# Linear attention over block means: means of the normed rows and one folded product for keys and for values, in place of means of keys and values

## The chip, the cores and the metric

One Trainium2 chip, and one of its cores. The kernel is one launch that runs a whole stack of layers on 2048 rows of 128 numbers. The time is the device time of one execution in microseconds (us); the profiled execution is a separate one, with its own time. Before the change the median of three runs was 4840.54 us (4836.08 to 4840.71).

## The reference

The change touches one layer of the stack, called Hale in the kernel (the eleventh of its 14 stages), and of it the global half; x below are the normalised rows. Cut to what matters:

```python
q = heads(x @ Wq.T); k = heads(x @ Wk.T); v = heads(x @ Wv.T)      # 16 heads of 8
local_out = local_attention(q, k_loc, v_loc, min(local_window, N))
glob = chunked_causal_linear_attention(q, k, v, chunk=chunk_size)   # level 0
scale_w = jax.nn.softmax(haar_scale)
for lvl in range(num_levels):                                       # levels 1 to 4
    block = 2 ** (lvl + 1)                                          # 2, 4, 8, 16
    k_lvl = causal_block_mean(k, block) @ haar_Wk[lvl].T
    v_lvl = causal_block_mean(v, block) @ haar_Wv[lvl].T
    glob = glob + scale_w[lvl] * chunked_causal_linear_attention(q, k_lvl, v_lvl, chunk=chunk_size)
diff = local_m - glob_m
gate_h = silu(concatenate([x, diff]) @ Wg.T + bg)
alpha = sigmoid(gate_h @ Wgo.T + bgo)
return (alpha * local_m + (1.0 - alpha) * glob_m) @ Wo.T + bo
```

causal_block_mean replaces row i by the mean of the rows from the start of its block up to i. The linear attention puts q and k through elu + 1 (phi), and divides each output by the sum of its weights, at least a small constant. Means, Wk and haar_Wk are all linear, and the mean acts on rows while the weights act on columns, so their order is free.

## The kernel before

*Blocks and units.* The 2048 rows are four blocks b of 512 (BW). The class HaleLinear, after the local attention, works in 20 units (b, l), a block and a level 0 to 4, in that order (`run`). Two generators are stepped against each other: `scores` of a unit, which yields after each of its 8 score tiles, and `keys` of the next unit, stepped once at each of those yields, twice in a level 4 unit, where the next unit's `keys` also has to make the next block's queries. A third, `mix`, which makes gate and output of a finished block, is stepped through the level 0 and 1 units of the block after. A scheduler of the framework turns this order into each engine's queue and may advance an instruction past others; an engine then runs its queue strictly in order.

*keys(b, l).* At level 0 `queries` comes first: three matmuls of the high and low parts (mm3, L148 to L150), phi (L2008 to L2013, then the split into hl_pqh and hl_pql, L142 and L143), DMAs that lay these out for the heads (hl_qs, L2031), and v in natural layout, hl_nat (L2036 to L2038), from which the values of level 0 are copied (L2071). The keys of level 0 are mm3 of the normed rows with Wk. The keys of the levels 1 to 4 are mm3 with hl_wl, the product of Wk and haar_Wk made once at the start (L1957 to L1965), which leaves unaveraged keys of the level in PSUM. A segmented scan on DVE (L2076, with a 0/1 tile hl_seg that restarts the sum at a block's first row) turns these to running sums, hl_km; POOL divides by the count (L2079, hl_inv). Then a yield, phi on hl_km, and 12 DMAs that lay the keys out in hl_KS. The values of a level: `mean` multiplies hl_nat by the averaging matrix hl_avg (L2055) and ACT copies the result (L2057); after the yield that follows phi, four matmuls with hl_bdv, the block-diagonal haar_Wv (L2089), and a copy to hl_V (L2090). Another yield, then four transposes of the keys (L2094), their copy hl_kn (L2096), a yield, and for each of the four chunks of 128 rows: the state's increment (L2103), the product of queries and state so far (L2109), its copy (L2110), the increment masked on DVE (hl_t, L2112, single buffer) and added to the state on POOL (hl_S, L2113).

*scores(b, l).* For four groups g of four heads and two pairs of chunks i2: two score matmuls to a PSUM tile ps_a of which two exist (L2155), masked to the causal part either on DVE (L2163) or, for i2 = 0 of g 0 and 2, by another matmul (L2157) and a Relu on ACT (L2160); then, two tiles later, 8 matmuls with the values (`av`, L2142; the trace lists an fp32 matmul like these as two). After two groups the sums are copied by ACT (hl_u, L2126), transposed (`fin2`, L2132) and added to hl_st on DVE (L2135). At the end DVE takes the maximum with 1e-6 and the reciprocal (hl_r, L2180 and L2181), at the levels 1 to 4 times the level's weight (L2183), and hl_o is the product (L2190), which POOL adds to the block's hl_glob (L2191). In a level 4 unit the next block's queries are spread to hl_QP, one product for each head of a group, on ACT for three groups (L2047) and on DVE for the last (L2049).

*PSUM.* The tag c, used by mm3 and the state's increments, has one bank, the tags b and m share three, a has two tiles of two banks.

Of the kernel before, what the change touches and what calls it, by code (L numbers as in the profile page):

```python
# [13 lines left out]
F32 = mybir.dt.float32  # L14
# [7 lines left out]
P = 128  # L22
# [151 lines left out]
class Stage:  # L174
# [75 lines left out]
    def normed(self, b, key="ln"):  # L250
# [11 lines left out]
        xn = self.lnp.tile([P, 4, P], F32, name=key + "_xn", bufs=1)  # L262
# [19 lines left out]
    lnx = 2  # L282
# [1521 lines left out]
class Hale(Attn16):  # L1804


    lnx, NQ = 4, 2
# [140 lines left out]
class HaleLinear:  # L1948
# [3 lines left out]
    def __init__(self, c, stage):  # L1952
# [4 lines left out]
        wkr = c.load(st, "hl_wkr", (P, P), ins["h_wkr"])  # L1957
        bdk = c.load(st, "hl_bdk", (P, 4, P), ins["h_bdk"])
        pw = c.ps("b")
        nc.tensor.matmul(pw, wkr, bdk.rearrange("p l d -> p (l d)"), start=True, stop=True)  # L1960
        wl = [wp.tile([P, 4, P], F32R, name=f"hl_wl{k}") for k in range(2)]
        raw = st.tile([P, BW], F32, name="hl_wlr")
        nc.scalar.copy(raw, pw)
        c.split(*(t.rearrange("p l d -> p (l d)") for t in wl), raw)
        self.wl = wl  # L1965
# [10 lines left out]
        self.seg = c.load(wp, "hl_seg", (P, 4, BW), ins["h_seg"], dtype=BF16)  # L1976
        self.inv = c.load(wp, "hl_inv", (P, 4, 16), ins["h_inv"])
        self.bdv = c.load(wp, "hl_bdv", (P, 4, P), ins["h_bdv"])
# [41 lines left out]
    def queries(self, b):  # L2020
# [12 lines left out]
        pn = c.ps("m")  # L2033
        for i in range(4):
            s = slice(i * P, (i + 1) * P)
            nc.tensor.matmul(pn[:, s], self.lns[b]["xT"][:, s], self.wvn, start=True, stop=True)  # L2036
        t = wk.tile([P, 4, P], F32, name="hl_nat")
        nc.scalar.copy(t.rearrange("p t d -> p (t d)"), pn)  # L2038
        self.nat[b] = t
# [11 lines left out]
    def mean(self, x, l):  # L2051
        c, nc = self.c, self.c.nc
        pm = c.ps("m")
        for i in range(4):
            nc.tensor.matmul(pm[:, i * P : (i + 1) * P], x[:, i, :], self.avg[:, l, :], start=True, stop=True)  # L2055
        t = self.wk.tile([P, BW], F32, name="hl_mean", bufs=1)
        nc.scalar.copy(t, pm)  # L2057
        return t

    def keys(self, b, l):  # L2060
# [4 lines left out]
        nat, phq = self.nat[b], self.phq[b]  # L2065
        (V, Vh), KS = self.VL[self.n % 2], self.KS[self.n % 2]
        self.n += 1
        pk = c.ps("c")
        if l == 0:
            c.mm3(pk, self.wk_, ln["hl"])  # L2070
# [14 lines left out]
        if l:  # L2085
            yield
            pv = c.ps("m")
            for i in range(4):
                nc.tensor.matmul(pv[:, i * P : (i + 1) * P], vm[:, i * P : (i + 1) * P], self.bdv[:, l - 1, :], start=True, stop=True)  # L2089
# [347 lines left out]
```

## Time and profile before

| what | us |
|---|---|
| median of three runs | 4840.54 |
| profiled execution, its own time | 4829.24 |
| its span, first to last instruction | 4827.3 |
| stretch of HaleLinear in it | about 3195 to 3620 |
| from one unit to the next, block 0 | 17.5 |
| from one unit to the next, levels 2 and 3 of later blocks | 17.8 |
| level 1 of later blocks, beside the tail of mix | 18.9 |
| level 4 and the next level 0 together | 41.3 |

Over the whole span the profile lists PE (TensorE's matmuls) with PEld (its weight loads, which overlap them), DVE (VectorE), ACT (ScalarE), POOL (GpSimd) and SP (the engine that issues the DMAs). The groups give for one line, engine, operation and tile the busy time and mean duration of one instruction, and then the time that the engine stood idle just before, with what ended it. A part of the waits says who waited for whom, how long in total, how often, and the longest. The chain of waits follows the work that ended last back from its end: each piece is what the next one waited for, or ran behind on the same engine. By the chain of the whole span, PE has 68% of it and DVE 21%. In the steady part of the stretch the granted TensorE clock is 1.00 of full speed; in its first 20 us it is 0.61.

### The profile page before, as it was taken

What the parts mean: (1) busy time and instruction counts of PE and PEld (TensorE: products, weight loads), DVE (VectorE), ACT (ScalarE), POOL (GpSimd) and SP (SyncE); (2) the same over time, 40 slices, a digit from 0 to 9 for tenths busy, and PEclk for the clock granted to TensorE, in tenths of its full rate; (3) what the DMA queues carried; (4) which work ended last, traced back from release to release, by engine and by line L of the source; (5) the groups of instructions that cost most, each with busy time, mean ns of one, the idle gap of its engine ahead of it and who ended that gap; (6) DMA issues with size and microseconds to landing.
All of it is one profiled execution on the core that took longest, in us unless ns stands there. A gap on an engine that the chain in (4) does not pass through costs nothing.

```text
span 4827.3 us, 89159 instructions
## 1 busy us (share of the span) xinstructions
PE 4397.6 (91%) x36369; PEld 2493.9 (52%) x36388; DVE 3709.7 (77%) x5694; ACT 3052.3 (63%) x5570; POOL 947.1 (20%) x826
## 2 busy tenths in 40 slices
PE   5979999988699988799999999989988989999998
PEld 4744444655344443463444447756656634444466
DVE  7867887589666654789999958447868879999777
ACT  4634568875355555356888875345546648888866
POOL 4730000554100000330000013012215600000056
PEclk9966899998699999898999999989999969999999
DMA  1010000000000000000000000112211000000000
GB/s 52 4 47 6 4 2 9 23 1 17 17 14 14 18 10 8 8 1 2 2 2 2 2 4 12 33 50 51 52 47 37 9 8 2 2 2 2 2 20 7
DMA packets 69484, 73.33 MB, mean 15 GB/s; under 512 B 17616, under 2 KB 44102, under 8 KB 69076
## 3 DMA queue, kind: packets, MB, share of 16 engines
q1 hardware_dynamic: 69076, 67.64, 5.0%
q8 instruction: 287, 4.70, 0.4%
q14 instruction: 121, 0.99, 0.1%
HBM read 32.09 MB, written 1.05 MB: 7 GB/s over the span
## 4 chain that ended last, share of the span: by engine, by line
PE 68%; DVE 21%; ACT 5%; issue 4%; POOL 1%; DMA 1%; SPq 0%; POOLq 0%; ACTq 0%; DVEq 0%
PE ps_c L874 15%; PE ps_a L824 10%; PE ps_c L1478 5%; DVE at_mx L828 4%; PE ps_b L895 4%; PE ps_c L878 3%; PE ps_a L1438 3%; PE ps_b L1491 3%; PE ps_b L148 2%; PE ps_a L148 2%; PE ps_a L150 2%; PE ps_b L149 2%; PE ps_a L149 2%; PE ps_b L150 2%; DVE m_hl L450 1%
## 5 line engine op out<-in xcount | busy, mean ns | idle before, releaser
L901 ACT ACTIVATE at_P<-ps_b 128x512 f32<-128x512 f32 (+2 forms) x2688 | 1414.4, 581 | 333.7 <-PE ps_b L895 205.6
L828 DVE TENSOR_REDUCE at_mx<-ps_a 128x2 f32<-128x1024 f32 (+2 forms) x1344 | 1537.0, 1183 | 103.7 <-PE ps_b L895 60.2
L874 PE MATMUL ps_c<-at_P,at_V 128*32 128x256 f32 (+3 forms) x10752 | 865.8, 395 | 7.8 <-ACT at_u L883 7.3
L895 PE MATMUL ps_b<-at_q,at_KT 32*128 32x512 f32 (+2 forms) x2688 | 761.0, 499 | 6.6 <-DMA at_q<-at_mT 5.0
L824 PE MATMUL ps_a<-at_KT,at_q 32*128 32x512 f32 (+3 forms) x2688 | 701.5, 522 | 46.9 <-DVE at_mx L828 44.7
L824 PEld LDWEIGHTS ps_a<-at_KT,at_q 32*128 32x128 f32 x2688 | 267.5, 196 | 494.1 <-issue 331.9
L449 ACT ACTIVATE m_hh<-ps_a,moe_b 128x512 fp32r<-128x512 f32 x512 | 350.0, 689 | 193.0 <-DVE m_h L446 160.5
L1439 DVE TENSOR_REDUCE ml_mx<-ps_a 128x2 f32<-128x1024 f32 x256 | 305.0, 1221 | 214.0 <-PE ps_a L1438 213.3
L450 POOL TENSOR_TENSOR m_hl<-m_h,m_hh 128x512 fp32r<-128x512 f32 x256 | 360.2, 1408 | 541.1 <-ACT m_hh L449 531.9
L1493 ACT ACTIVATE ml_P<-ps_b 128x512 f32<-128x512 f32 (+1 forms) x544 | 272.4, 576 | 229.8 <-PE ps_b L1491 227.6
L874 PEld LDWEIGHTS ps_c<-at_P,at_V 128*32 128x32 f32 x10752 | 215.9, 110 | 358.8 <-issue 179.9
L878 PE MATMUL ps_c<-wide,zerob 128*32 128x256 bf16 x5184 | 390.2, 281 | 0.0
L261 POOL TENSOR_TENSOR ln_rs<-ln_ve,nhalf 128x4 f32<-128x4 f32 x56 | 61.6, 1101 | 1656.2 <-DVE ln_ve L259 1647.6
L895 PEld LDWEIGHTS ps_b<-at_q,at_KT 32*128 32x128 f32 x2688 | 326.8, 189 | 74.1 <-issue 44.2
L450 DVE TENSOR_TENSOR m_hl<-m_h,m_hh 128x512 fp32r<-128x512 f32 x256 | 256.9, 1004 | 80.1 <-ACT m_hh L449 78.8
L448 ACT ACTIVATE m_h<-ps_a,moe_b 128x512 f32<-128x512 f32 x320 | 220.7, 690 | 75.3 <-DVE m_hl L450 39.9
L1478 PE MATMUL ps_c<-ml_P,ml_V 128*33 128x512 f32 (+3 forms) x1088 | 253.5, 588 | 2.9 <-ACT ml_P L1493 2.9
L148 PE MATMUL ps_b<-m_hh,moe_w2h 128*128 128x512 f32 x512 | 221.2, 432 | 20.7 <-DVE m_t L470 19.2
L149 PE MATMUL ps_b<-m_hl,moe_w2h 128*128 128x512 f32 x512 | 213.2, 416 | 25.5 <-DVE m_hl L450 20.0
L148 PE MATMUL ps_a<-ln_h,moe_w1h 128*128 128x512 f32 x512 | 219.1, 429 | 11.8 <-ACT m_hh L449 11.7
L878 PEld LDWEIGHTS <-zerob 128*32 128x32 bf16 x5184 | 155.8, 100 | 112.6 <-issue 9.2
L149 PE MATMUL ps_a<-ln_l,moe_w1h 128*128 128x512 f32 x512 | 206.6, 403 | 0.0
(655 smaller groups left out, 7734.6 us busy)
## 6 DMA issues: line engine op xcount, KB each, us to landing
hl_KS<-hl_pkh SPq DMA_DIRECT2D x160, 64.0 KB
moe_w_raw<-in_l0f_W SPq DMA_DIRECT2D x32, 256.0 KB
ml_pad<-ml_QT SPq DMA_DIRECT2D x32, 256.0 KB
moe_w_raw<-in_l3f_W SPq DMA_DIRECT2D x32, 256.0 KB
hl_KS<-hl_pkl SPq DMA_DIRECT2D x80, 64.0 KB
at_pad<-at_q SPq DMA_DIRECT2D x64, 64.0 KB
at_q<-at_mT SPq DMA_DIRECT2D x192, 4.0 KB
at_cosT<-in_cosT SPq DMA_DIRECT2D x8, 256.0 KB
```

The lines of the kernel that those rows point to most:

```text
L148: nc.tensor.matmul(out, lh, rh, start=start, stop=False)
L149: nc.tensor.matmul(out, lh, rl, start=False, stop=False)
L449: nc.scalar.activation(hh, ph, AF.Relu, bias=bias)
L450: (nc.gpsimd if f in ((0, 2) if self.spare else MS) else nc.vector).tensor_tensor(hl, h, hh.bitcast(F32), ALU.subtract)
L824: self.in_turn(nc.tensor.matmul(pa[:, k, :w], q[r, i * P : (i + 1) * P], KT[r, ch * BW : ch * BW + w], start=True, stop=True))
L828: nc.vector.tensor_reduce(mx[:, i, 2 * jj : 2 * jj + 2, ch], pa[:, :, :w], AX.X, ALU.max)
L874: self.in_turn(nc.tensor.matmul(self.acc[32 * j : 32 * j + 32, s], self.V[:, kt, h : h + 32], ps[j][:, s], start=start, stop=stop))
L878: self.in_turn(nc.tensor.matmul(self.acc[32 * j : 32 * j + 32, z], c.zerob, c.wide[:, z], start=False, stop=False))
L895: self.in_turn(nc.tensor.matmul(pbs[k][:, off:end], KT[r, kt * P : (kt + 1) * P], q[r, off:end], start=True, stop=not diag))
L901: nc.scalar.activation(p[:, off:end], pbs[k][:, off:end], AF.Exp, scale=scale)
L1439: nc.vector.tensor_reduce(mx[:, i, :, ch], pa, AX.X, ALU.max)
L1478: self.in_turn(nc.tensor.matmul(self.acc[64 * j : 64 * j + m, s], v, ps[k][j][:, s], start=kt + k == 0, stop=kt + k == NT - 1))
```

## The change

It is one edit of HaleLinear with two helpers. The running means are now taken of the normed rows xn, which the layer norm keeps for all four blocks (lnn = 4 buffers of ln_xn instead of 1), with hl_avg: `means` copies the PSUM result twice on ACT, as the high part hl_meanh (new L2051) and in full (hl_mean, new L2052), and subtracts on DVE for the low part hl_meanl (new L2053). There is a yield after it. The keys of a level are mm3 of these with hl_wl, and go straight to phi; the values are one product of the mean with hl_wvl (new L2075), the product of Wv and haar_Wv, made at the start as hl_wl is. Level 0 has its values from xT and Wv by the same lines, without hl_nat. The scan, hl_seg, POOL's product, hl_inv, and the load of hl_bdv in its old place are gone. The weight of a level moves from hl_r into hl_o, which becomes a product with a scalar and a tensor (new L2179). The loads of the two folds and of Wq and Wk come first.

```diff
@@ -259,7 +259,7 @@
         nc.vector.tensor_scalar_add(ve, mv[:, :, 1], EPS)
         rs = self.sm.tile([P, 4], F32, name=key + "_rs")
         nc.gpsimd.tensor_tensor(rs, ve, c.nhalf, ALU.pow)
-        xn = self.lnp.tile([P, 4, P], F32, name=key + "_xn", bufs=1)
+        xn = self.lnp.tile([P, 4, P], F32, name=key + "_xn", bufs=self.lnn)
         for i in range(4):
             nc.vector.tensor_scalar(xn[:, i, :], c.x[:, 4 * b + i, :], mv[:, i, 0:1], rs[:, i : i + 1], ALU.subtract, ALU.mult)
         return xn
@@ -279,7 +279,7 @@
             r["hl"] = (h, l)
         return r
 
-    lnx = 2
+    lnx, lnn = 2, 1
 
     def top2(self, l, shape=(P, 4, E)):
         c, nc = self.c, self.c.nc
@@ -1804,7 +1804,7 @@
 class Hale(Attn16):
 
 
-    lnx, NQ = 4, 2
+    lnx, lnn, NQ = 4, 4, 2
 
     def open(self):
         c, ins = self.c, self.c.ins
@@ -1954,15 +1954,17 @@
         nc, ins = c.nc, c.ins
         wp = self.wp = stage.pool("hl_w")
         st = stage.pool("hl_s", 2)
-        wkr = c.load(st, "hl_wkr", (P, P), ins["h_wkr"])
-        bdk = c.load(st, "hl_bdk", (P, 4, P), ins["h_bdk"])
-        pw = c.ps("b")
-        nc.tensor.matmul(pw, wkr, bdk.rearrange("p l d -> p (l d)"), start=True, stop=True)
-        wl = [wp.tile([P, 4, P], F32R, name=f"hl_wl{k}") for k in range(2)]
-        raw = st.tile([P, BW], F32, name="hl_wlr")
-        nc.scalar.copy(raw, pw)
-        c.split(*(t.rearrange("p l d -> p (l d)") for t in wl), raw)
-        self.wl = wl
+        raw = {}
+        for n in "kv":
+            w = c.load(st, "hl_wr", (P, P), ins[f"h_w{n}r"])
+            bd = c.load(st, "hl_bd", (P, 4, P), ins[f"h_bd{n}"])
+            pw = c.ps("b")
+            nc.tensor.matmul(pw, w, bd.rearrange("p l d -> p (l d)"), start=True, stop=True)
+            raw[n] = (st if n == "k" else wp).tile([P, 4, P], F32, name=f"hl_w{n}l")
+            nc.scalar.copy(raw[n].rearrange("p l d -> p (l d)"), pw)
+        self.wl = [wp.tile([P, 4, P], F32R, name=f"hl_wl{k}") for k in range(2)]
+        c.split(*self.wl, raw["k"])
+        self.wvl = raw["v"]
         self.wq = c.load_hl(wp, st, "hl_wq", (P, P), ins["h_wq"])
         self.wk_ = c.load_hl(wp, st, "hl_wk", (P, P), ins["h_wk"])
         stage.shut("hl_s")
@@ -1973,9 +1975,6 @@
         self.bgo = c.load(wp, "hl_bgo", (P, 1), bcast(ins["h_bgo"]))
         self.wo = c.load(wp, "hl_wo", (P, P), ins["h_wo"])
         self.bo = c.load(wp, "hl_bo", (P, P), bcast(ins["h_bo"]))
-        self.seg = c.load(wp, "hl_seg", (P, 4, BW), ins["h_seg"], dtype=BF16)
-        self.inv = c.load(wp, "hl_inv", (P, 4, 16), ins["h_inv"])
-        self.bdv = c.load(wp, "hl_bdv", (P, 4, P), ins["h_bdv"])
         self.avg = c.load(wp, "hl_avg", (P, 4, P), ins["h_avg"])
         self.bdm = c.load(wp, "hl_bdm", (P, 16, 9), ins["h_bdm"])
         self.tri = c.load(wp, "hl_tri", (P, P), ins["h_tri"])
@@ -2030,13 +2029,6 @@
             for s, src in enumerate((qh, qh, ql)):
                 nc.sync.dma_start(t[32 * s : 32 * s + 32, :].bitcast(F32), src[32 * g : 32 * g + 32, :].bitcast(F32))
         self.phq[b] = phq
-        pn = c.ps("m")
-        for i in range(4):
-            s = slice(i * P, (i + 1) * P)
-            nc.tensor.matmul(pn[:, s], self.lns[b]["xT"][:, s], self.wvn, start=True, stop=True)
-        t = wk.tile([P, 4, P], F32, name="hl_nat")
-        nc.scalar.copy(t.rearrange("p t d -> p (t d)"), pn)
-        self.nat[b] = t
         yield
 
     def spread(self, g):
@@ -2048,46 +2040,45 @@
             return
         nc.vector.tensor_tensor(self.QP[g], self.qs[g].bitcast(F32).unsqueeze(1).to_broadcast([P, 4, BW]), self.hm.unsqueeze(2).to_broadcast([P, 4, BW]), ALU.mult)
 
-    def mean(self, x, l):
-        c, nc = self.c, self.c.nc
+    def means(self, xn, l):
+
+        c, nc, wk = self.c, self.c.nc, self.wk
         pm = c.ps("m")
         for i in range(4):
-            nc.tensor.matmul(pm[:, i * P : (i + 1) * P], x[:, i, :], self.avg[:, l, :], start=True, stop=True)
-        t = self.wk.tile([P, BW], F32, name="hl_mean", bufs=1)
-        nc.scalar.copy(t, pm)
-        return t
+            nc.tensor.matmul(pm[:, i * P : (i + 1) * P], xn[:, i, :], self.avg[:, l, :], start=True, stop=True)
+        h, l = (wk.tile([P, BW], F32R, name=f"hl_mean{k}", bufs=1) for k in "hl")
+        x = wk.tile([P, BW], F32, name="hl_mean", bufs=1)
+        nc.scalar.copy(h, pm)
+        nc.scalar.copy(x, pm)
+        nc.vector.tensor_tensor(l, pm, h.bitcast(F32), ALU.subtract)
+        return x, (h, l)
 
     def keys(self, b, l):
         c, nc, wk = self.c, self.c.nc, self.wk
         if l == 0:
             yield from self.queries(b)
         ln = self.lns[b]
-        nat, phq = self.nat[b], self.phq[b]
+        phq = self.phq[b]
         (V, Vh), KS = self.VL[self.n % 2], self.KS[self.n % 2]
         self.n += 1
+        if l == 0:
+            x, hl, w, wv = ln["xT"], ln["hl"], self.wk_, self.wvn
+        else:
+            x, hl = self.means(ln["xn"], l - 1)
+            w, wv = tuple(t[:, l - 1, :] for t in self.wl), self.wvl[:, l - 1, :]
+            yield
         pk = c.ps("c")
-        if l == 0:
-            c.mm3(pk, self.wk_, ln["hl"])
-            nc.scalar.copy(Vh[:, :, :, 0:8], nat.rearrange("p t (h d) -> p t h d", d=8))
-        else:
-            c.mm3(pk, tuple(t[:, l - 1, :] for t in self.wl), ln["hl"])
-            vm = self.mean(nat, l - 1)
-            km = wk.tile([P, BW], F32, name="hl_km", bufs=1)
-            nc.vector.tensor_tensor_scan(km, self.seg[:, l - 1, :], pk, 0.0, ALU.mult, ALU.add)
-            pk = km
-            k3 = km.rearrange("p (n s) -> p n s", s=16)
-            nc.gpsimd.tensor_tensor(k3, k3, self.inv[:, l - 1, :].unsqueeze(1).to_broadcast([P, BW // 16, 16]), ALU.mult)
+        c.mm3(pk, w, hl)
+        pv = c.ps("m")
+        for i in range(4):
+            s = slice(i * P, (i + 1) * P)
+            nc.tensor.matmul(pv[:, s], x[:, s], wv, start=True, stop=True)
+        nc.scalar.copy(Vh[:, :, :, 0:8], pv.rearrange("p (t h d) -> p t h d", t=4, d=8))
         yield
         phk, kh, kl = self.phi(pk, "hl_pk")
         for g in range(4):
             for s, src in enumerate((kh, kl, kh)):
                 nc.sync.dma_start(KS[g][32 * s : 32 * s + 32, :].bitcast(F32), src[32 * g : 32 * g + 32, :].bitcast(F32))
-        if l:
-            yield
-            pv = c.ps("m")
-            for i in range(4):
-                nc.tensor.matmul(pv[:, i * P : (i + 1) * P], vm[:, i * P : (i + 1) * P], self.bdv[:, l - 1, :], start=True, stop=True)
-            nc.scalar.copy(Vh[:, :, :, 0:8], pv.rearrange("p (t h d) -> p t h d", t=4, d=8))
         yield
         pt = c.ps("m")
         for i in range(4):
@@ -2179,19 +2170,17 @@
         r = wk.tile([P, 4, 16], F32, name="hl_r")
         nc.vector.tensor_scalar_max(r, st[:, :, :, 8], 1e-6)
         nc.vector.reciprocal(r, r)
-        if l:
-            nc.vector.tensor_scalar_mul(r, r, self.w[:, l - 1 : l])
         bc = r.unsqueeze(3).to_broadcast([P, 4, 16, 8])
         if l == 0:
             self.glob = wk.tile([P, 4, 16, 8], F32, name="hl_glob")
             nc.vector.tensor_tensor(self.glob, st[:, :, :, 0:8], bc, ALU.mult)
         else:
             t = wk.tile([P, 4, 16, 8], F32, name="hl_o", bufs=1)
-            nc.vector.tensor_tensor(t, st[:, :, :, 0:8], bc, ALU.mult)
+            nc.vector.scalar_tensor_tensor(t, st[:, :, :, 0:8], self.w[:, l - 1 : l], bc, ALU.mult, ALU.mult)
             nc.gpsimd.tensor_tensor(self.glob, self.glob, t, ALU.add)
 
     def run(self):
-        self.done, self.phq, self.nat = {}, {}, {}
+        self.done, self.phq = {}, {}
         units = [(b, l) for b in range(NB) for l in range(5)]
         for _ in self.keys(*units[0]):
             pass
@@ -2407,10 +2396,8 @@
     i64 = np.arange(64)[None]
     k128 = np.arange(P)[:, None]
     d["h_maskc"] = np.ascontiguousarray(np.stack([np.where(k128 <= i64, 0.0, -1e30), np.where((k128 <= 64 + i64) & (k128 > i64), 0.0, -1e30)], 1).astype(ml_dtypes.bfloat16))
-    d["h_wkr"] = g("L3_attn_a_Wk")
+    d["h_wkr"], d["h_wvr"] = g("L3_attn_a_Wk"), g("L3_attn_a_Wv")
     t512 = np.arange(BW)[None]
-    d["h_seg"] = np.ascontiguousarray(np.broadcast_to(np.stack([(t512 % B > 0) for B in (2, 4, 8, 16)], 1), (P, 4, BW)).astype(ml_dtypes.bfloat16))
-    d["h_inv"] = f(np.broadcast_to(np.stack([1.0 / (t512[:, :16] % B + 1) for B in (2, 4, 8, 16)], 1), (P, 4, 16)).astype(np.float32))
     d["h_hm"] = f((row[:, None] // 8 == np.arange(4)[None]).astype(np.float32))
     return d
```

## The prediction

> **What bounds the kernel now.** I read the busy shares first, then the busy time by stretch, the groups of the linear-attention stretch, its waits, and the chain of waits through one unit. Line numbers are those of the kernel before; lines of the changed kernel are called new.
>
> ```profile
> span 4827.3 us, 89159 instructions
> ...
> PE 4397.6 (91%) x36369; PEld 2493.9 (52%) x36388; DVE 3709.7 (77%) x5694; ACT 3052.3 (63%) x5570; POOL 947.1 (20%) x826
> ```
>
> PE is busy for 91% of the span. The change touches one stretch only, from 3195 to 3620 us, 9% of the span. The stretches inside it (us; busy us of PE, PE's weight loads, DVE, ACT, POOL; clock; DMA):
>
> ```profile
> core 0: us, PE busy (x) PEld busy (x) DVE busy (x) ACT busy (x) POOL busy (x), PEclk, DMA share, GB/s
> 3195.00:3215.00 20.00, 9.17 (x26) 5.89 (x26) 9.07 (x20) 7.25 (x13) 12.07 (x23) 0.61 0.46 130
> ...
> 3340.00:3420.00 80.00, 73.63 (x822) 50.77 (x821) 65.00 (x102) 43.04 (x76) 18.29 (x24) 1.00 0.21 51
> ```
>
> In the steady part PE is busy 92%, DVE 81%, ACT 54%, POOL 23%. So at most 8% of some 400 us is PE's idle time there, and only the first 20 us are slack. What lies in that idle time shows in the groups (count, busy us and mean ns, then idle before):
>
> ```profile
> L2163 DVE TENSOR_TENSOR hl_am<-ps_a,hl_tri 128x1024 f32<-128x1024 f32 x120 | 146.0, 1216 | 20.6 <-PE ps_a L2155 20.1
> ...
> L2079 POOL TENSOR_TENSOR hl_km<-hl_km,hl_inv 128x512 f32<-128x512 f32 x16 | 22.3, 1396 | 66.0 <-DVE hl_km L2076 53.1 <-DVE hl_r L2180 13.0
> ...
> L2076 DVE TENSOR_TENSOR_SCAN hl_km<-hl_seg,ps_c 128x512 f32<-128x512 bf16 x16 | 19.5, 1217 | 1.9 <-PE ps_c L150 1.9
> ...
> L143 DVE TENSOR_TENSOR hl_pkl<-hl_pk,hl_pkh 128x512 fp32r<-128x512 f32 x19 | 12.9, 679 | 1.9 <-ACT hl_pkh L142 1.9
> ...
> L2183 DVE TENSOR_SCALAR hl_r<-hl_r,hl_sc 128x64 f32<-128x64 f32 x16 | 9.9, 621 | 0.4
> L2057 ACT COPY hl_mean<-ps_b 128x512 f32<-128x512 f32 x16 | 9.3, 584 | 9.9 <-PE ps_b L2055 9.9
> ```
>
> and in the waits (us in total, times, longest):
>
> ```profile
> PEld ps_a L2155 <- DVE hl_am L2163: 21.0, 34, 1.1
> ...
> PE ps_a L2155 <- DVE hl_am L2163: 11.2, 21, 0.9
> ```
>
> The chain that ended last, through the start of one unit (start, us, what):
>
> ```profile
> 3357.61 0.53 DVE hl_st L2135 x2
> ...
> 3358.38 1.15 DVE hl_km L2076
> 3359.53 0.46 DVE hl_r L2181
> ...
> 3360.01 0.99 DVE hl_r L2183
> 3360.99 1.13 DVE hl_am L2163
> 3362.13 0.60 DVE hl_o L2190
> 3362.72 0.34 DVE hl_e L2011
> 3363.06 1.14 DVE hl_am L2163
> ...
> 3364.25 0.50 PE ps_a L2155
> ```
>
> A unit (one block, one level) takes 17.8 us between the same instructions of successive units. DVE carries its first 6.6 us, because the score matmuls L2155 wait for DVE's mask to free their PSUM. PE carries the other 11.2. Summing PE's spacings, I find about 16.0 us of work per unit, so 1.6 to 1.85 us is stall. That is the most an ordinary unit can give.
>
> **The change, part by part.** *Removed*, once per unit of levels 1 to 4, so 16 times: the scan, 16 x 1.217 = 19.5 us of DVE; the product with hl_inv, 22.3 us of POOL; the weight on hl_r, 9.9 us of DVE. In the ordinary unit two of the three stand on the chain above, 1.15 and 0.99 us.
>
> *Added*: the subtraction that makes the low part of the mean (new L2053). No row has this shape with a PSUM source. Between L2135 (PSUM, 144 elements, 0.297) and L2163 (PSUM, 1024, 1.216) a line gives 0.68 for 512; L143, the same operation from SBUF, takes 0.679; I take 0.69, so 16 x 0.69 = 11.0 of DVE. A second ACT copy of the mean, 16 x 0.584 = 9.3. PE's work per unit stays the same: four matmuls for the mean, three for the keys, four for the values, in both. The weight now rides in hl_o, a product with two tensors and a scalar like L2013 (0.677), against 0.683 before.
>
> DVE has 29.4 - 11.0 = 18.4 us less work. If it all came off the path, and the POOL step as well, the gain would be near 30 us.
>
> *Moved*: the mean now stands ahead of the keys, so the chain is mean, ACT copy, key matmuls, phi, where it was key matmuls, scan, POOL, phi. Phi comes a step later in the generator. I walked the changed kernel's order of instructions on each engine with these durations. For an ordinary unit, times run from its first score matmul:
>
> - fin2 ends at 1.6, hl_st on DVE at 2.15, hl_r 2.9, then the second mask until 4.1 (6.2 before, in the unit that starts at 3373.76). hl_o to 4.8, the new subtraction to 5.5, the next masks to 6.7 and 7.9. The third pair's scores, which wait for the first of these, start at about 6.8; before, 8.3. So 1.5 us of the old stall is gone.
> - The mean's matmuls end at 2.4, its ACT copies at 3.05 and 3.65. The last key matmuls wait for the subtraction, until 5.55, and end at 6.3. ACT's two steps of phi end at 7.6, DVE's at 9.0 or a little later (before, 8.85). Keys are thus no earlier, in spite of all that was removed.
> - Then DVE's queue has hl_pk, a mask, hl_pkl, a mask, and only then hl_t (L2112), which frees the one ps_c bank that the next state matmul (L2103) needs. Before, hl_t stood before that last mask. The mask ends at 12.1 to 12.5, hl_t at 12.4 to 12.9; PE, done with all else at 11.4 to 11.7, idles 1.1 to 1.2 us, and 0.35 to 0.6 more for POOL's addition to hl_S (0.49, L2113) behind it.
> - Sum: stall 1.5 to 1.85 again, unit 17.6 to 17.8 against 17.8. I take -0.1, for nine units of this kind (of 20: 3 in the first block, 2 in each other): -0.9.
>
> What is late next, then, is hl_t behind a mask. Its cover before was that mask's later place.
>
> *The three units of level 4 with the queries of the next block, and the level 0 after each* (together 41.3 us before). ACT multiplies hl_QP there (12 x 0.715), with the copy hl_u behind. In the new order the next queries' hl_pq comes after a mask (7.3 against 5.8), the keys' hl_pk at 13.4 against 9.7, and ACT's row of hl_QP is cut by hl_pkh and hl_kn, so that the last hl_u ends near 22.6 against 19.9 and its transposes 2.75 later. In the level 0 unit that follows, ACT no longer waits 2.6 for POOL's product ahead of its mask. The gate's matmul L2239 is 3.1 late, but scores and state matmuls have gone ahead meanwhile: +1.3 for the pair (-1 to +4), three times: +3.9.
>
> *The three level 1 units with the tail of mix* (18.9 before): the key matmuls wait for the addition to x that frees ps_c; I find 18.5 to 20: +0.5 each, +1.5.
>
> *The start*: the wanted weights are now loaded first, before the last attention is over; SP issues a load each 0.47 us, and five stood ahead of hl_wkr. The query matmuls start at about 3198.5 instead of 3200.79. ACT no longer does hl_nat between two steps of phi. And the product on POOL, 3.23 us there at 3220.83, ahead of ACT's first mask, is gone, where PE stood for 6.5 us; the new mean and keys take its place in part. The second fold costs two matmul halves and a copy, 0.58 on ACT, in idle time. I take -2.8 (0 to -6). *The end*: the last unit has nothing beside it and loses the weight, 0.24 to 0.6: -0.4.
>
> Sum: -0.9 + 3.9 + 1.5 - 2.8 - 0.4 = **+1.3 us**. The profiled execution took 4829.24 (span 4827.3), which would become 4830.5. It is 11.3 below the median of the runs, 4840.54, so the forecast there is **4842**, no change. About 0.2%, 9.7 us, is what a measurement of this kernel can tell from no change.
>
> **A rule against the change.** The rows: ACT is busy 54%, and its 0.58 for a copy from PSUM lies in idle time in my walk. The Trainium skill, "Trainium Kernel Development and Optimization", section "Best Practices", warns to mind PSUM pressure, that is evacuation. The mean is read from PSUM three times instead of once; if those reads stood on the path they would cost 16 x (0.58 + 0.69), some 20 us.
>
> **Rivals.**
>
> *A, the stall stays gone.* DVE gets to the masks 1.5 us earlier and the new wait for hl_t is shorter than I find, because hl_t is ready before the mask or the mask comes early enough. For: two removed steps stood on the chain. Against: the new order puts that mask ahead. Then each of 12 ordinary and level 1 units gains up to 1.5, 18 us; with the other terms as above (+3.9 - 2.8 - 0.4) that is -17.3: 4823. Half of it gives 4832.
>
> *B, the longer key chain decides; slower.* Mean, two copies, subtraction, keys, phi: if the subtraction is held behind hl_o and a mask (1.2), hl_pk, its transposes and every hl_t move back by as much, and PE, which has nothing else left by 11.7, idles that much longer. It decides once hl_pk ends after 9.7. At +1.0 in 12 units and +2.7 in the three level 4 units, whose whole delay I counted as half recovered: 12 + 8 - 3 = +17: 4858. Against: the subtraction needs no more than ACT's copy at 3.65, long past when its turn comes.
>
> **How the numbers follow.** Forecast 0.42, within about 8 us of 4842; A 0.28; B 0.30. The bounds: ordinary units -14 to +10, level 4 pairs -3 to +12, level 1 units -3 to +6, start 0 to -6; not all at one end, so some 20 each way: **4820 to 4862**. Faster 0.30 (most of A, and a little of the forecast), within 0.2% 0.38, slower 0.32.
>
> **What would show it.** In the changed profile: the third pair's scores start near 6.8 in a unit (if 8.3, the gain was not there); PE's idle time before L2103 named with hl_t, 1 us and more per unit (if near zero, A); hl_pk ends near 9 to 9.3 in a unit (if 10 or more, B); the level 4 unit's last hl_u near 22.6; the first mask of ACT ends 2 to 4 us earlier than 3228.26. The forecast is wrong if units shrink below 17.0 or grow above 18.5.

## The result, and the profile after

The changed kernel takes 4856.77 us in the median (4850.83 to 4861.43, six runs), the kernel before 4834.93 (4829.03 to 4840.71, six runs). The ratio is 1.0045, 95% interval 1.0035 to 1.0055: slower by about 22 us. The forecast was 4842, no change; the time lies inside the range of 4820 to 4862, near the price of rival B, but "no change" was wrong.

The page of the kernel after; below its span, each engine's busy time, share and instructions. The profiled execution took 4859.93 us.

```profile
span 4858.2 us, 89145 instructions
...
PE 4440.9 (91%) x36390; PEld 2514.1 (52%) x36390; DVE 3694.2 (76%) x5678; ACT 3057.3 (63%) x5583; POOL 928.5 (19%) x810
```

DVE has 15.5 us less work than before and POOL 18.6 less, as the change meant. PE has 43.3 us *more*, with 21 more matmul records of 36,000. Part of that lies elsewhere in the span, which ran at a lower mean clock (0.921 against 0.926). To leave that out I use one measure from here on: *linear time*, from the last transposes of the local attention to the last addition to x. It was 424.8 us and is 446.4: +21.6, as much as the difference of the medians. It is read, like all units below, from one profiled execution of each kernel.

The busy time of the kernel after by stretch (us; busy us of PE, PE's weight loads, DVE, ACT, POOL; clock; DMA):

```profile
3345.00:3402.00 57.00, 54.80 (x592) 37.44 (x594) 40.33 (x68) 25.83 (x50) 7.96 (x13) 1.00 0.17 42
3195.00:3625.00 430.00, 391.75 (x3998) 263.01 (x3997) 289.67 (x498) 215.58 (x385) 73.29 (x119) 0.95 0.20 50
```

And the kernel before, over the same 430 us:

```profile
3195.00:3625.00 430.00, 371.79 (x3993) 256.65 (x3993) 314.41 (x557) 217.22 (x385) 96.52 (x138) 0.94 0.21 53
```

Over three units of block 1, levels 1 to 3, at a full clock in both kernels, DVE's load fell from 81% (3338 to 3391 before) to 71%, and PE's rose from 94% to 96%. PE is busy 20.0 us longer over the 430 us, with 5 more records of 4000. Three groups of the kernel after in that stretch (count, busy us and mean ns, then idle before) show what of the walk came true:

```profile
L2146 PE MATMUL ps_a<-hl_QP,hl_KS 128*128 128x512 f32 x320 | 123.1, 469 | 3.0 <-DVE hl_am L2154 2.8
L2133 PE MATMUL ps_b<-hl_am,hl_V 128*32 128x128 f32 x2560 | 112.5, 281 | 1.4 <-DVE hl_am L2154 1.3
...
L2053 DVE TENSOR_TENSOR hl_meanl<-ps_b,hl_meanh 128x512 fp32r<-128x512 f32 x16 | 10.9, 683 | 4.8 <-ACT hl_mean L2052 4.8
```

And its waits (us in total, times, longest):

```profile
PEld ps_c L2094 <- DVE hl_t L2103: 12.6, 18, 1.2
...
PEld ps_a L2146 <- DVE hl_am L2154: 6.8, 13, 0.9
```

The prices of the new instructions were nearly right: the subtraction 0.683 (0.69 forecast), and by rows not shown the second copy 0.594 (0.584) and hl_o 0.744 (0.677). So was the main effect: the score matmuls' wait for DVE's mask, 21.0 us for the weight loads and 11.2 for the matmuls before, is 6.8 and 2.8, and the wait for hl_t that was named as next is there, 12.6 us for 3.6 before, 1.2 at its longest. The surprise is the value matmuls L2133. There are as many as before (2560), of the same mean, yet they cover 112.5 us. Their row before was:

```profile
L2142 PE MATMUL ps_b<-hl_am,hl_V 128*32 128x128 f32 x2560 | 100.0, 279 | 0.4 <-DVE hl_am L2163 0.4
```

The chain of waits through one ordinary unit of the kernel after (block 1, level 3, from 3383.14 to 3402.31; start, us, what) shows how:

```profile
3389.22 0.34 PE ps_b L2133 x2
3389.56 0.43 PE ps_c L149
3389.99 0.24 PE ps_c L150
3390.22 0.57 PE ps_b L2133 x14
...
3393.16 0.56 PE ps_b L2133 x10
3393.71 0.58 PE ps_b L2085 x4
3394.30 0.25 PE ps_b L2100 x2
3394.54 0.35 PE ps_b L2133 x6
...
3395.59 0.29 DVE hl_am L2154
3395.88 0.85 issue
3396.73 0.31 DVE hl_t L2103
...
3397.08 0.53 PE ps_c L2094 x2
```

Before, the first 6.6 us of such a unit were a chain of DVE instructions. Now nearly every piece is PE's own; the one stall is from 3395.56 to 3397.08, 1.5 us, for the mask and hl_t. And two groups of value matmuls are torn, with the last parts of the key product (L149) and the transposes of the keys (L2085) between their pieces: 2 + 14 records take 0.34 + 0.57, and 10 + 6 take 0.56 + 0.35. A whole group, 16 records, is one piece of 0.57. (A third group is cut 2 + 14 near the end of the unit, but its first two records follow the run before, so no run is added; with what lies between, its pieces take 2.51 us, as the whole ones do in joined below.) In the whole stretch the value matmuls come in 158 runs against 139 before; in an ordinary unit in 9 against 7. That is the scheduler's order: the same value matmuls, placed differently.

The units, from the first score matmul to that of the next (us; a range where units differ), with those of the main experiments:

| part | before | after | joined | joined_pair | split | w_in_o | w_in_o_old | ahead3 |
|---|---|---|---|---|---|---|---|---|
| start to first unit of level 1 | 48.8 | 44.5 | 44.0 | 44.1 | 49.5 | 48.7 | 47.8 | 44.7 |
| block 0, levels 1 to 3 | 17.5 | 18.6 | 17.7 | 17.7 | 18.2 | 17.5-17.8 | 17.5-19.5 | 17.1-17.7 |
| level 1 | 18.9 | 20.6 | 20.0 | 20.0 | 19.7 | 18.9 | 18.9 | 18.6 |
| levels 2 and 3, blocks 1 and 2 | 17.8 | 19.2 | 18.2 | 18.2 | 18.5 | 17.9 | 18.1 | 17.3-17.6 |
| level 4 and next level 0 | 41.3 | 44.2-44.9 | 44.0-45.0 | 43.3-43.8 | 41.9-43.1 | 43.3-44.3 | 41.0-42.6 | 42.5 |
| last unit to x | 35.9 | 35.7 | 35.7 | 35.7 | 36.9 | 35.7 | 35.7 | 36.4 |
| linear time | 424.8 | 446.4 | 435.5 | 432.3 | 437.9 | 433.3 | 431.5 | 421.3 |

The pairs can't be read from this table as they stand. TensorE's granted clock was 0.50 for 6.8 us in each of the three level 4 units of the kernel after; the stretches (columns as before):

```profile
3311.50:3318.30 6.80, 6.13 (x21) 4.73 (x20) 1.92 (x5) 4.18 (x9) 1.50 (x4) 0.50 0.44 106
3417.30:3424.10 6.80, 6.69 (x52) 5.52 (x56) 2.20 (x7) 4.86 (x11) 1.96 (x4) 0.50 0.37 90
3519.70:3526.50 6.80, 6.33 (x34) 4.91 (x38) 1.75 (x6) 4.59 (x11) 1.95 (x4) 0.50 0.41 98
```

All three pairs of joined have one as well (6.8, 6.8 and 3.4 us), two of w_in_o and one each of joined_pair, split and w_in_o_old (3.4 us each); the pairs of the kernel before and of ahead3 have none. Where a run has pairs with and without, a stretch of 3.4 us goes with 0.5 to 1.6 us more. The pairs without one take 41.3 before, 43.4 in w_in_o, 41.0 in w_in_o_old, 43.3 in joined_pair, 41.9 in split and 42.5 in ahead3. For the kernel after and joined there is no such pair, and what theirs would be is not shown; nor is whether the change brings the stretches on.

### The profile page after: what moved, and what is told of

It is laid out like the page before. It is cut to its first block, busy times and chain, and to the rows that moved or that the text cites. A ratio compares the mean times of both kernels' runs of the same rounds, so it can differ in the third digit from the quotient of the medians.

```text
span 4858.2 us, 89145 instructions
## 1 busy us (share of the span) xinstructions
PE 4440.9 (91%) x36390; PEld 2514.1 (52%) x36390; DVE 3694.2 (76%) x5678; ACT 3057.3 (63%) x5583; POOL 928.5 (19%) x810
## 4 chain that ended last, share of the span: by engine, by line
PE 59%; DVE 14%; ACT 4%; issue 3%; POOL 1%; DMA 1%; SPq 0%; POOLq 0%; DVEq 0%; ACTq 0%
PE ps_c L874 12%; PE ps_a L824 8%; PE ps_c L1478 5%; PE ps_a L1438 3%; PE ps_b L1491 3%; PE ps_b L895 3%; DVE at_mx L828 2%; PE ps_c L878 2%; PE ps_b L2133 2%; PE ps_a L148 1%; PE ps_a L2146 1%; PE ps_a L150 1%; PE ps_a L149 1%; PE ps_b L148 1%; PE ps_b L149 1%
## 5 line engine op out<-in xcount | busy, mean ns | idle before, releaser
L895 PEld LDWEIGHTS ps_b<-at_q,at_KT 32*128 32x128 f32 x2688 | 325.5, 188 | 74.2 <-issue 43.8
L448 ACT ACTIVATE m_h<-ps_a,moe_b 128x512 f32<-128x512 f32 x320 | 220.8, 690 | 78.5 <-DVE m_hl L450 42.5
L148 PE MATMUL ps_b<-m_hh,moe_w2h 128*128 128x512 f32 x512 | 222.5, 435 | 20.7 <-DVE m_t L470 17.8
L149 PE MATMUL ps_b<-m_hl,moe_w2h 128*128 128x512 f32 x512 | 214.4, 419 | 25.2 <-DVE m_hl L450 19.5
L878 PEld LDWEIGHTS <-zerob 128*32 128x32 bf16 x5184 | 155.5, 100 | 112.5 <-issue 9.1
L149 PE MATMUL ps_a<-ln_l,moe_w1h 128*128 128x512 f32 x512 | 208.4, 407 | 0.0
```

The costliest lines, as they stand in the source:

```text
L148: nc.tensor.matmul(out, lh, rh, start=start, stop=False)
L149: nc.tensor.matmul(out, lh, rl, start=False, stop=False)
L878: self.in_turn(nc.tensor.matmul(self.acc[32 * j : 32 * j + 32, z], c.zerob, c.wide[:, z], start=False, stop=False))
L895: self.in_turn(nc.tensor.matmul(pbs[k][:, off:end], KT[r, kt * P : (kt + 1) * P], q[r, off:end], start=True, stop=not diag))
```

## The experiments

Three causes were weighed at first: the order of PE's queue, that is the torn runs; L, the longer key chain (mean, copies, subtraction, keys, phi) that now stands in line within a unit; and V, the evacuation, PSUM read three times for a mean. The expectations call the first theory O. To hold an order I add dependences without semaphores between the instructions of one engine, in the sequence of a written list, so that the scheduler can't exchange them; each queue then has exactly that order and no new wait. The kernels below were timed in five rounds on three chips; ratios are to the kernel before on the same chip, with 95% intervals.

**joined.** The changed kernel, its queues held to their own order but for one thing: each group of 8 value matmuls stays whole, at the place of its last piece (the edit is shortened).

```diff
+ORDERS = (PE, DVE, ACT, POOL)          # instruction numbers, one list an engine
+for names in ORDERS:
+    for a, b in zip(names, names[1:]):
+        tc.add_manual_dep(at[b], a, NoSync, reason="order")
```

> The changed kernel with one thing different: in TensorE's queue the eight value matmuls of a group (new L2133), which the changed kernel cuts up and sets between other matmuls, stand together again, each group at the place of its last piece. That makes 130 runs of value matmuls instead of 152. The queues of DVE, ACT and POOL are held to the changed kernel's order. Theory O (the order: a run of value matmuls costs TensorE some 0.3 us to go in and out of, as the spacings show, 0.20 out of it and 0.1 into it): 22 runs less, 5 to 9 us faster than the changed kernel, ordinary units 19.17 to about 18.5 us. Theory L (the key chain is longer through mean, copies and subtraction, and TensorE waits for hl_t): within 2 us of the changed kernel. Theory V (the mean's three reads of PSUM cost ACT and DVE time on the path): within 2 us too.

Measured: 4847.52 us, ratio 1.0022 (1.0006 to 1.0037); linear time 435.5, half of the loss gone, somewhat more than theory O had expected; 136 runs. The same place in the chain of joined, in the same columns:

```profile
3382.47 0.23 PE ps_c L149
3382.70 0.24 PE ps_c L150
3382.94 0.57 PE ps_b L2149 x16
...
3385.88 0.44 PE ps_b L2101 x4
3386.31 0.25 PE ps_b L2116 x2
3386.56 0.57 PE ps_b L2149 x16
...
3388.12 0.85 issue
3388.97 0.31 DVE hl_t L2119
```

In the kernel after, the first torn group cost 0.34 more in itself, and 0.20 more in what followed its first piece (L149 0.43 against 0.23); the second cost 0.34 and 0.14 (the transposes 0.58 against 0.44). Together 1.02, and an ordinary unit is 1.0 shorter. The wait behind mask and hl_t is as long as it was. So the torn groups are half of the loss, nearly all of it in the units of levels 1 to 3, and the rest is something else.

**split.** The opposite, on the kernel before, with its queues held: 64 groups of value matmuls that stood whole behind a pair of score matmuls are cut in the middle. In outline:

```diff
-scores scores value x8
+scores value x4 scores value x4
```

> The kernel before with one thing different: 64 groups of eight value matmuls (L2142), each right behind a pair of score matmuls, are cut in halves that stand behind one score matmul each. Same matmuls, same data, 202 runs of value matmuls instead of 138; the queues of DVE, ACT and POOL are held to the order of before. Theory O: 64 x 0.3 = 19 us at most, 10 to 19 since about half of the cuts lie where TensorE waits for DVE in any case. Theories L and V have no cost in this: 0 to 3 us, for the scores that come a quarter of a us later.

Measured: 4850.00 us, ratio 1.0030 (1.0018 to 1.0041); linear time 437.9, +13.1 for 64 more runs, 0.20 each, within what theory O expected. (One pair has a stretch of half clock, some 1.2 of the 13.1.) Nothing of the change is in this kernel, and it is slower by more than half of what the change cost. In its chain one cut group, with the scores:

```profile
3377.10 0.23 PE ps_a L2171
3377.34 0.36 PE ps_b L2158 x8
3377.69 0.43 PE ps_a L2171
3378.13 0.36 PE ps_b L2158 x8
```

This is 1.38 us, where the chain of the kernel before has the same work whole:

```profile
3384.97 0.47 PE ps_a L2155 x2
3385.43 0.57 PE ps_b L2142 x16
```

That is 1.04, so a cut costs 0.34 where PE leads. Where DVE leads, in the first third of a unit, it is partly hidden, hence 0.20 in the mean.

**w_in_o.** The kernel before with the smallest part of the change alone: the weight moves from hl_r into hl_o, one DVE instruction of 0.62 less for each unit of levels 1 to 4.

```diff
-        if l:
-            nc.vector.tensor_scalar_mul(r, r, self.w[:, l - 1 : l])
-            nc.vector.tensor_tensor(t, st[:, :, :, 0:8], bc, ALU.mult)
+            nc.vector.scalar_tensor_tensor(t, st[:, :, :, 0:8], self.w[:, l - 1 : l], bc, ALU.mult, ALU.mult)
```

> The kernel before with one part of the change alone: the level's weight goes into hl_o (a product with a scalar and a tensor) and its own multiplication on hl_r is gone. Scan and POOL's product stay. By the chain of waits of before it is worth up to 0.7 us in an ordinary unit and less in the others: 3 to 8 us faster than before. If TensorE's order alone sets the time (theory O), 0 to 3 us faster, as the order hardly changes (133 runs). L and V say nothing of this.

Measured: 4842.10 us, ratio 1.0016 (1.0005 to 1.0027); linear time 433.3, +8.5: slower, where 0 to 8 us faster had been expected. Nearly all of it lies in the pairs of level 4 and level 0, which grow from 41.3 to 43.4 at full clock (44.3 in the two with a stretch of half clock). DVE's timeline at the start of a level 4 unit (start, us, what, idle before) tells why:

```profile
3401.74 0.42 DVE L2011 TENSOR_SCALAR hl_e<-hl_e 128x512 f32<-128x512 f32 x1
3402.08 1.22 DVE L2163 TENSOR_TENSOR hl_am<-ps_a,hl_tri 128x1024 f32<-128x1024 f32 x1
3403.21 0.68 DVE L2013 SCALAR_TENSOR_TENSOR hl_pq<-ps_c,hl_e 128x512 f32<-128x512 f32 x1
```

In the kernel before, hl_pq stands ahead of that mask:

```profile
3396.70 0.68 DVE L2013 SCALAR_TENSOR_TENSOR hl_pq<-ps_c,hl_e 128x512 f32<-128x512 f32 x1
3397.30 1.22 DVE L2163 TENSOR_TENSOR hl_am<-ps_a,hl_tri 128x1024 f32<-128x1024 f32 x1
```

With one instruction fewer the scheduler put the mask first, and the next queries, the keys behind them and the last copies all come later. The ordinary units gain nothing either: 17.9 for 17.8. There the scheduler put hl_o ahead of the mask and beside POOL's product, and it takes 1.50 us instead of 0.74.

**w_in_o_old.** The same, with each queue held to the order of the kernel before. In outline:

```diff
+ORDERS = (those of the kernel before, without the instructions on hl_r)
```

> The same instructions as in the run with the weight in hl_o alone, but with the queues of TensorE, DVE, ACT and POOL held to the order of the kernel before (less the 16 multiplications). In that run the pairs of level 4 and the next level 0 took 44.3 us against 41.3 before, although only the weight was moved; its DVE queue has the next queries' hl_pq behind a mask, and ACT's row of hl_QP starts before hl_pkh and hl_kn. Theory O (the scheduler's new order, not the instructions): pairs back at 41 to 41.5, ordinary units 17.0 to 17.8, the stretch of linear attention 424.8 us or less, so the kernel 0 to 8 us faster than before. Rival Q (the product with scalar and tensor itself, 0.745 against 0.683, or its place on DVE, makes the pairs long): pairs stay at 44, the stretch near 433.

Measured: 4837.72 us, ratio 1.0014 (1.0001 to 1.0028). The pairs are 41.0 again, the two that the clock left alone, so their loss in w_in_o was the order, not the instruction. This rests on units: in the whole kernel the gain that was expected is not there, and the ratio can't be told from that of w_in_o, 1.0016. (The profiled execution is the slowest of the twelve and had four stretches of half clock in the units between the first and the last, one of them in the third pair; its linear time, 431.5, counts them.) But the ordinary units are 18.1, no better than before. DVE's timeline in one of them:

```profile
3403.29 1.03 DVE L2027 TENSOR_SCALAR hl_e<-hl_e 128x512 f32<-128x512 f32 x1 [0.62 <-ACT hl_e L2025]
```

And POOL's timeline at the same time:

```profile
3402.75 1.28 POOL L2205 TENSOR_TENSOR hl_glob<-hl_glob,hl_o 128x512 f32<-128x512 f32 x1 [0.82 <-DVE hl_o L2204]
```

POOL's addition starts earlier, since hl_o does, and now lies over DVE's hl_e, which takes 1.03 where it takes 0.42 alone. The 0.99 of the weight on hl_r in the prediction's chain was of the same kind: 0.24 in a level 4 unit, where POOL was still. What the removal freed in these two runs was a collision, and the next instruction had it.

**joined_pair.** Joined, and in the three level 4 units also the DVE, ACT and PE queues as the kernel before had them (hl_pq, hl_pql and hl_pk one mask earlier, the key's steps on ACT ahead of the row of hl_QP).

```diff
-mask hl_pq mask hl_pql mask hl_e mask hl_pk
+hl_pq mask hl_pql mask hl_e hl_pk mask
```

> The changed kernel with groups of value matmuls joined, as before, and in the three level 4 units also the order of before on DVE (hl_pq, hl_pql and hl_pk each one mask earlier), on ACT (the masks and hl_pkh, hl_u and hl_kn ahead of the row of hl_QP) and on TensorE (the next keys' matmuls ahead of the third pair's scores, the key transposes ahead of the last scores). Theory O: pairs fall from 44.6 to 41.3 to 42, the stretch from 435.5 to 425 to 428 us, level with the kernel before: nothing of the change's own instructions is slower, its order was. Theory L or V: the pairs stay above 44, the stretch at 433 to 436.

Measured: 4842.50 us, ratio 1.0016 (1.0004 to 1.0028); linear time 432.3. The pairs are 0.7 to 1.3 shorter than in joined, but two of the three also lost their stretch of half clock; the two that have one of 3.4 us, the third of joined and the first here, differ by 0.3. The 41.3 to 42 of theory O is missed: at full clock the pairs take 43.3. With both orders mended 7.5 us of linear time remain, and the start alone is 4.7 better than before, so the units still lose 12: 0.1 to 0.4 in each ordinary unit, 1.1 in each at level 1, 1.2 to 1.7 in each at level 0, and 0.2 in a level 4 unit at full clock. In the chain of a level 0 unit of this kernel:

```profile
3418.31 0.36 PE ps_c L149
3418.67 0.25 PE ps_c L150
...
3418.95 0.61 ACT hl_e L2023
...
3419.57 0.64 ACT hl_e L2024
...
3420.24 0.44 DVE hl_e L2026
...
3420.70 0.70 DVE hl_pk L2028
...
3421.45 1.12 PE ps_c L2235 x2
```

The last row is the gate's matmul of mix. It waits for the one bank ps_c, which the keys hold until hl_pk has read them; and L149 had waited 0.3 for the mean's low part. Before, the scan freed the bank with one instruction, 1.15 us. So it is theory L in part, and in part the bank, held through phi: the gate's first matmul starts 8.7 to 9.5 into this unit here and in the kernel after, 4.3 in the kernel before, and still 8.8 in ahead below, where the means are ready early; the level 0 units of ahead take 21.4 for 20.4 before.

**ahead, ahead2, ahead3.** The changed kernel with the means of the next level made one unit earlier, inside the keys of this one: in ahead at their end, in ahead2 in the step of phi, in ahead3 after the transposes of the keys. The copies and the subtraction stay (ahead2 and ahead3 subtract from the copy in SBUF); the order is the scheduler's own.

```diff
-            x, hl = self.means(ln["xn"], l - 1)
+            x, hl = self.ahead
-            yield
...
+        if l < 4:
+            self.ahead = self.means(ln["xn"], l)
```

> The changed kernel with the means of a level taken at the end of the unit before, behind its states, so that keys and values start at once from ready means; the scheduler makes all queues anew (143 runs of value matmuls). ACT's two copies and DVE's subtraction are all still there. Theory L: hl_pk comes some 3 us earlier in a unit, the wait for hl_t goes, ordinary units 17 us or less, 10 us or more faster than the kernel before. Theory O: about half of the extra runs are gone and the scan too: ordinary units 17.3 to 18.2, near the kernel before. Theory V: stays within 5 us of the changed kernel.

> The changed kernel with the next level's means taken in the step of phi, a unit ahead of their use, and the low part of the mean subtracted from the copy in SBUF; scheduler's order. Without a mean in the unit, an ordinary unit with the means a unit ahead took 16.07 us, with it at the end 17.73. Theory O: here the mean's matmuls lie in the time in which TensorE waits for DVE's masks (0.8 us a unit), but the value groups are cut again (7 to 8 runs) and DVE gets the subtraction early: 16.6 to 17.8 us for an ordinary unit, the stretch 412 to 428 us. Theory L (the chain alone counts): 16.1 us and 405.

> As the run with the means in the step of phi, but one step later, behind the key transposes: 7 runs of value matmuls in an ordinary unit, the masks of DVE ahead of the subtraction, and the level 4 unit nearly in the order of before. Theory O: ordinary units 16.6 to 17.2, pairs 41 to 42.5, the stretch 408 to 418 us: 7 to 17 us faster than the kernel before. Theory V (two copies and a subtraction for each mean cost the path 1 us a unit): ordinary units 17.5 or more, no faster than before.

Measured: ahead 4837.71 us, ratio 1.0001 (0.9992 to 1.0010), linear time 422.7; ahead2 4847.53, 1.0028 (1.0014 to 1.0043), 433.1; ahead3 4834.26, 1.0002 (0.9992 to 1.0011), 421.3. Two of the three undo the whole loss; none is faster than the kernel before, which theory L had expected of ahead and theory O of ahead3, and ahead2 is slower than both its forecasts. PSUM is read as often as in the changed kernel (ahead) or once less (ahead3), so V, the evacuation as work, is not what cost the 22 us: with as many copies off the chain the time is back. These runs change the order too (150, 149 and 144 runs of value matmuls), so they don't separate theory L from O. The ordinary units of ahead3, 17.3 to 17.6, are for the first time shorter than before's 17.8, and level 1 too, 18.6 against 18.9. In ahead the levels without a mean in their unit, level 3, run in 16.1 and the level 2 units in 17.7 to 17.8 (blocks 1 to 3): a mean in the unit, with the order that it brings, costs 1.7 there. Ahead2 differs from ahead3 by the place of one call. Its pairs take 44.6 at full clock and 47.0 and 47.4 with stretches of half clock, instead of 42.5; why the 44.6 is long is open.

**ahead4.** Ahead3 with PE's queue held to an order without torn groups: 121 runs instead of 144, the unit's last group at the end of the unit, and the transposes fin2 whole ahead of the key matmuls. In outline:

```diff
-value x2 state state value x14
+state state value x16
```

> As the run with the means behind the key transposes, with its DVE, ACT and POOL queues kept, and TensorE's changed in three ways: each group of value matmuls whole; a unit's last group at the unit's end and not behind the next unit's first score matmul; the transposes fin2 whole ahead of the key matmuls. Theory O: the start of an ordinary unit is then that of the 16.07 us unit, which has no mean, and the mean at its place cost 0.3; 16.1 to 16.7 us for an ordinary unit (17.3 to 17.6 in the run it is made from, 17.8 before), level 1 units 18 to 18.6, pairs as there, 42.5; the stretch 407 to 413 us against 424.8 before: 12 to 17 us faster than the kernel before. If TensorE's order is worth no more than its cut groups, 2 runs of 17: 0.6 us a unit, the stretch 413 to 416.

Measured: 4833.42 us, ratio 1.0002 (0.9991 to 1.0013), linear time 421.4: no better than ahead3, and the expectation is missed. Ordinary units came to 16.9 to 17.4 (one 17.7), and a pair to 42.7, of which the level 0 unit is one us longer than in ahead3. The end of an ordinary unit in its chain:

```profile
3367.54 0.48 PE ps_a L2163 x2
...
3368.11 1.24 DVE hl_am L2171
...
3369.39 0.64 PE ps_b L2150 x16
```

With the last group held at the end, PE has nothing to do while its mask is made, 1.4 us; in ahead3 no wait stands there. A longer run costs a wait where its data come late. No version beats the kernel before measurably: the best linear times are 3.5 us shorter than its own, 0.07% of the whole, and the intervals of the ratios hold 1.

## Where the prediction failed, and what of it held

That the time lies inside the range, and beside rival B's price, is luck: the terms that were walked give no change, and half of the 22 us came from a term that was put at nothing. The step that failed is "PE's work per unit stays the same": the instructions are the same, their order is not. The prediction took 16.0 us of work and 1.5 to 1.85 of stall for an ordinary unit, 17.6 to 17.8 in sum. The unit is 19.17, of which the chain puts 1.5 down to the stall, as forecast; PE's own pieces are 17.6. Joined shows 1.0 of the gap to be the two torn groups; the other 0.6 is partly that 16.0 was low from the start: by its busy time PE works 16.6 of the 17.8 us in the unit of before that starts at 3373.76 (18.3 in the unit of the kernel after, 17.3 in joined). DVE's queue was walked to within 0.2 us (the second mask ends at 4.3 for 4.1, the subtraction at 5.5 as forecast). The torn groups could have been counted in the changed order of PE's instructions; the walk followed waits and took PE's work as given.

The terms, in us for the linear time:

| term | forecast | measured | what the runs show |
|---|---|---|---|
| ordinary units, 9 | -0.9 | +11.4 | about 9 of it the torn groups (joined); the rest not isolated |
| pairs of level 4 and level 0 | +3.9 | +9.6 | late hl_pq, hl_pk and hl_u as walked; the level 0 unit too; a stretch of half clock in each |
| level 1 units, 3 | +1.5 | +5.2 | 1.8 torn groups (joined); 3.4 put down to L, not isolated |
| start | -2.8 | -4.3 | weights and first keys earlier |
| end | -0.4 | -0.25 | |
| sum | +1.3 | +21.6 | |

- *The third pair's scores, near 6.8.* By the trace these are the fifth of the unit's eight score tiles, the first of its third group. They start at 7.6 (3390.72), and no mask holds them: the chain there is all PE. The old stall went, as forecast: the waits of the score matmuls for DVE's masks fell by 22.6 us. Its gain went into PE's longer queue.
- *hl_pk near 9 to 9.3.* In ordinary units it ends at 9.6, under the 9.7 from which rival B was to decide; in joined at 9.0, and those units are still longer than before. So for these B hit the price, 4858, by another road. At level 1 hl_pk does end late, at 12.2 for 9.9, as B would have it; the 12 us that remain in the units of joined_pair are its key chain and the bank, in shares that no run tells apart.
- *The wait for hl_t, 1.1 to 1.2 and POOL's addition.* From 3395.56 to 3397.08, with the mask ahead of hl_t, as walked.
- *The pairs.* hl_pk ends at 12.7 in the unit against 9.7 before (13.4 forecast), the last hl_u between 23.7 and 24.3 (22.6 forecast; the 19.9 that the prediction gives for before is its start, it ended at 20.4), with half clock in between. The prediction let half of the delay be recovered in level 0; instead the level 0 unit is itself 0.9 to 1.6 longer, since the gate's matmul waits for ps_c. Of the +2.9 to +3.5 a pair, w_in_o has +2.0 at full clock with nothing changed but the weight (there hl_pk ends at 12.75 and the last hl_u at 22.7), and holding the order takes that back. In the changed kernel holding it takes back little that the clock does not explain (joined_pair).
- *Start.* ACT's first mask ends 31.0 after the last transposes against 33.9: 2.9 earlier, inside the 2 to 4 forecast, and the first unit is shorter by another 1.4.
- *The weight.* 9.9 us of DVE counted as removed were, for the most part, a collision with POOL's product with hl_inv. With that product kept (w_in_o, w_in_o_old) a collision moved to the next instruction; in the kernel after the product is gone too, and hl_o (0.74) and hl_e (0.43) run at their short times.
- *The most it could give.* The "near 30 us" is not the sum of its terms: 18.4 and 22.3 make 40.7. Nothing else rests on it.
- *The rule on PSUM pressure.* The reads as such are not what costs: ahead has all three and is level with before.

Open: the 0.4 in an ordinary unit of joined is put down to L because ahead3 has units below before's, but no run changed that alone; the same holds for the rest at level 1. How much of the pairs' loss in the kernel after is order, bank or half clock is not shown either, and ahead2's long pairs are not explained.

## What to carry to other kernels

Where a scheduler writes the queues, count in the new order the places at which TensorE changes from one kind of tile to another, not only the instructions; on this kernel such a change cost 0.3 to 0.5 us, and a run with the order held to the old one helps to tell whether an edit or its order is slow. Take a step that only feeds the next unit out of that unit's chain and make it a unit earlier, where its chain has a unit of time to run. An instruction that is long only because another engine runs beside it may not be worth its length when it is removed: look at the shortest of its kind, and at what else runs then.

## What the runs showed of the hardware

- **A change of tile on TensorE.** The value matmuls use 128 x 32 weights, all others here 128 x 128. A whole group of 16 takes 0.57, two groups in a row 1.01; behind one, the first other matmul takes 0.2 more (scores 0.43 or 0.66 for one or two, against 0.23 and 0.47). In split a cut cost 0.34. The Trainium skill, "TensorEngine Tiling (Array Packing)", section "Tiling Modes", says that changing the tiling mode drains TensorE. The chains of split and joined agree with that; the prices are for fp32.
- **DVE beside POOL.** DVE instructions that touch only SBUF took longer while POOL ran: hl_e 1.03 for 0.42, hl_o 1.50 for 0.74, the weight on hl_r 0.99 for 0.24. Where hl_e began first, with POOL's addition over its last 0.26, it took 0.41 (kernel before). In the two rows of w_in_o_old hl_e ends at 4.3 and POOL's addition at 4.0 (after 3400). The Trainium skill, "SBUF — State Buffer", section "SBUF: two separate sides", describes the shared port pair as an exclusive lock, held for a whole instruction. An hl_e that begins its 0.42 when POOL ends would end at 4.45, an estimate by that rule; the measured 4.3 is near it.
- **Half clock.** In the 18 units between the first and the last, TensorE's granted clock is 1.00 or 0.50, the latter in stretches of 3.4 or 6.8 us. In the profiled executions the kernel after has three of them (from 3311.5, 3417.3 and 3519.7) and the kernel before none; of 17 in all runs 12 lie in level 4 units. A value matmul's record is 421 ns long in one, 273 otherwise. A stretch of 3.4 us goes with 0.5 to 1.6 us in the unit or pair that has it.
